# A fifth load buffer for two passes of a Fourier-layer kernel, and a transposed tile that moves into the ring of rectified chunks

## The chip, the cores and the metric

The kernel runs on one core of a Trainium2 chip. The metric is the device time of one execution in microseconds (us); three executions of the kernel before give 11959.6, 11963.65 and 11971.61 us, so the median is 11963.65 us. One more execution was taken with the hardware profiler; the profile and every trace view below come from that one.

## What is computed

The reference takes 64 images of 256 x 256 points. Four Fourier layers turn each into 32 channels and mix them; then one transformer layer runs over the 256 rows of the image and 77 text tokens. Only the Fourier layers matter here:

```
v = [x, gx, gy] @ p_w + p_b                       # 32 channels, per point
for i in range(4):
    x_ft = rfft2(v)                               # only 12 y and 2*12 x frequencies are kept
    out1 = einsum('bixy,ioxy->boxy', x_ft[:, :, :12, :12], W1)
    out2 = einsum('bixy,ioxy->boxy', x_ft[:, :, -12:, :12], W2)
    x1 = irfft2(out_ft, s=(256, 256))
    x2 = einsum('bcxy,cd->bdxy', v, w_w[i]) + w_b[i]
    v = batch_norm(x1 + x2)                       # mean and variance over all 64 images
    if i < 3: v = relu(v)
```

The mean and variance are over the whole batch, so a layer cannot be finished for any image before its statistics are known for all of them. The kernel computes those from the frequencies and from the squares of the channel product, in a stage of its own.

## The kernel before

**Stages.** A first stage computes the frequencies of the input. Then come, three times, a mixing stage (`mix`, lines 392 to 493) and a pass over all images (`layer`, lines 508 to 750); a fourth mixing stage and the transformer end the kernel. A pass computes the layer's output for every image, rectifies it, writes it to DRAM, and transforms it forward for the layer after. Pass i = 0 rebuilds its input from the image itself; the passes i = 1 and i = 2, called the later passes here, read the channels that the pass before wrote, 8 MB an image, and write as much again.

**Chunks.** An image is worked on in eight chunks t = 0..7 of 128 partitions x 8 x 256 floats, 1 MB each. The order of all instructions in a pass is the order in which the code issues them (`tc.manual_schedule()`). Step (b, t) of the loop at lines 721 to 747 does:

- `pre(b, t)`: TensorE sums the inverse transform (line 616) and, in the later passes, the product of the loaded chunk `vin` with the weights (line 627) in PSUM. Half of the result is rectified by ScalarE (line 634) and half by VectorE (line 639; ScalarE at line 637 for t = 6) into a tile `vo`. SyncE issues the store of `vo` (line 640).
- in the later passes, `load_v`: SyncE issues the load of a later chunk into a tile `vin` (line 581). Its queue holds stores and loads in the order of the code.
- `product` of the chunk before (line 659), whose squares ScalarE sums (line 666).
- `turn(b, t)`: VectorE transposes `vo` into a tile `t32` (line 647).

**What lies between the chunks.** At t = 2 the products of chunks 0 and 1 are held back, and the forward transform along y of the image before (`along_y`, line 676) stands in their place: 256 matrix multiplies. Its PSUM result is read by VectorE and, by way of a copy `half` on ScalarE (line 686), by VectorE again (line 688): both transposes go into the tile `zt`. At t = 3 `along_x` (line 701) reads `zt`, and ScalarE and SyncE write the 72 KB of frequencies out (lines 708 and 709). `spread` (lines 598 and 602) runs at t = 3 and t = 5.

**Buffers.** A pool hands out its buffers in turn; a tile may be written when all users of the tile that had the buffer before are done. Pool `li` has two buffers of 16 KB a partition in pass 0, and four of 8 KB in the later passes (`vin`). Pool `lo` has four of 8 KB (`vo`). Pool `lz` holds one `zt` (8 KB) and one `half` (4 KB). Pool `lt` holds six `t32` (16 KB each). With the others they fill the SBUF nearly to its end. PSUM holds four tiles `ring` of two banks; `pre`, `product` and `along_y` take two tiles each, `spread` and `along_x` one.

**Between two passes.** The next mixing stage reuses the addresses. GpSimd issues the loads of the mixing weights into tiles `wn` (line 369), clears and fills part of the weight tile `wm` (lines 374 and 375), and issues the load of the frequencies of 56 images, `xh`, 4 MB (line 769), all on one queue in order. The order on that queue is chosen by the framework's scheduler, not written by hand. TensorE's first product of `mix` (line 419) needs `xh`.

Of the kernel before, what the change touches and what calls it, by code (L numbers as in the profile page):

```python
# [9 lines left out]
F32 = mybir.dt.float32  # L10
# [6 lines left out]
S = 256  # L17
C = 32
# [117 lines left out]
def tile_fno_fusion_transformer(ctx: ExitStack, tc: tile.TileContext, a, cst_d, grid_d, out):  # L136
# [371 lines left out]
    def layer(i, st, src, dst, acc):  # L508
# [7 lines left out]
        with ExitStack() as cx:  # L516
            def pool(name, bufs, **kw):
                return cx.enter_context(tc.tile_pool(name=name, bufs=bufs, **kw))

            ip = pool("li", 2 if i == 0 else 4, reuse_waits="tile")  # L520
            op, yp, cp, xp, zp, tp = (
                pool(n, k, reuse_waits="tile")
                for n, k in (("lo", 4), ("ly", 1), ("lc", 1), ("lx", 2), ("lz", 1), ("lt", 6))
# [39 lines left out]
            y_, t32, vin, vo = {}, {}, {}, {}  # L563

            def load_am(b):
                for n in range(2):
                    nc.sync.dma_start(
                        ams[b % 2][64 * n:64 * n + 2 * KX],
                        mix_d[i][b].rearrange("p k c -> (p k) c")[:, 512 * n:512 * n + 512],
                    )  # L570

            def load_x(b):
                for n in range(4):
                    nc.sync.dma_start(
                        mv[b % 2][32 * n + 24:32 * n + 28],
                        x[b].rearrange("(j n s) y -> n j s y", j=4, n=4)[n],
                    )

            def load_v(b, t):
                vin[b, t] = ip.tile([128, 8, S], F32, name="vin")  # L580
                nc.sync.dma_start(vin[b, t], src[b][:, t])
# [10 lines left out]
            def spread(b, h):  # L592

                y_[b, h] = yp.tile([128, 32, C], F32, name=f"y{h}")
                ps = pp.tile([128, 2, 512], F32, name="ring")
                for n in range(2):
                    hv = slice(64 * n, 64 * n + rows_)
                    nc.tensor.matmul(  # L598
                        ps[:, n, :], lhsT=EX[hv, 128 * h:128 * h + 128], rhs=ams[b % 2][hv],
                        start=True, stop=True, skip_group_check=True,  # L600
                    )
                nc.vector.transpose(  # L602
                    y_[b, h].rearrange("p q c -> p c q"), ps.rearrange("p n (c k) -> p (n c) k", k=32)
                )

            def four():

                t2 = [pp.tile([128, 2, 512], F32, name="ring") for _ in range(2)]
                return t2, [t2[n // 2][:, n % 2] for n in range(4)]

            def pre(b, t):
                t2, ps = four()
                for r in range(2):
                    for n in range(4):
                        q = 8 * (t % 4) + 4 * r
                        nc.tensor.matmul(  # L616
                            ps[n][:, 256 * r:256 * r + 256],
                            lhsT=y_[b, t // 4][32 * n:32 * n + K, q:q + 4, :].rearrange("p q c -> p (q c)"),
                            rhs=mv[b % 2][32 * n:32 * n + K, 2 * t + r, :] if i == 0 else T4[32 * n:32 * n + K, :],
                            start=r == 0, stop=i == 0, skip_group_check=True,  # L620
                        )
                if i:
                    v = vin.pop((b, t))
                    for k in range(4):
                        for n in range(4):
                            j = (n + k) % 4
                            nc.tensor.matmul(  # L627
                                ps[n][32 * j:32 * j + 32], lhsT=ws[32 * n:32 * n + 32],
                                rhs=v[32 * n:32 * n + 32, 2 * j:2 * j + 2, :], start=False, stop=True,
                                skip_group_check=True, tile_position=(32 * n, 32 * j),  # L630
                            )
                o = vo[b, t] = op.tile([128, 8, S], F32, name="vo")
                of = o.rearrange("p (n r) y -> p n (r y)", r=2)
                nc.scalar.activation(of[:, 0:2], t2[0], AF.Relu)  # L634

                if t == 6 or i == 0 and t == 1:
                    nc.scalar.activation(of[:, 2:4], t2[1], AF.Relu)  # L637
                else:
                    nc.vector.tensor_scalar(of[:, 2:4], t2[1], 0.0, None, ALU.max)  # L639
                nc.sync.dma_start(dst[b][:, t], o)  # L640

            def turn(b, t):

                o = vo[b, t]
                if t % 2 == 0:
                    t32[b, t // 2] = tp.tile([128, 8, 16, C], F32, name="t32")
                nc.vector.transpose(  # L647
                    t32[b, t // 2][:, :, 8 * (t % 2):8 * (t % 2) + 8, :].rearrange("p y s c -> p s y c"),
                    o.rearrange("p s (y l) -> p s y l", l=32),
                )  # L650

            def product(b, t):

                o = vo.pop((b, t))
                t2, ps = four()
                for k in range(4):
                    for n in range(4):
                        j = (n + k) % 4
                        nc.tensor.matmul(  # L659
                            ps[n][32 * j:32 * j + 32], lhsT=w4[i + 1][32 * n:32 * n + 32],  # L660
                            rhs=o[32 * n:32 * n + 32, 2 * j:2 * j + 2, :], start=True, stop=True,
                            skip_group_check=True, tile_position=(32 * n, 32 * j),
                        )
                for n in range(2):
                    at = 2 * (8 * b + t) + n
                    nc.scalar.activation(t2[n], t2[n], AF.Square, accum_out=acc[:, at:at + 1])  # L666

            zts = {}

            def along_y(b):  # L670
                t2, ps = four()
                for k in range(8):
                    for m in range(4):
                        for n in range(4):
                            j = (n + m) % 4
                            nc.tensor.matmul(  # L676
                                ps[n][32 * j:32 * j + 32], lhsT=FYT[32 * n:32 * n + 32, k, :],
                                rhs=t32[b, j][32 * n:32 * n + 32, k].rearrange("p s c -> p (s c)"),
                                start=k == 0, stop=k == 7, skip_group_check=True,
                                tile_position=(32 * n, 32 * j),  # L680
                            )
                for j in range(4):
                    t32.pop((b, j))
                zt = zts[b] = zp.tile([128, 2, 32, C], F32, name="zt")
                half = zp.tile([128, 2, 512], F32, name="half")
                nc.scalar.copy(half, t2[1])  # L686
                for h, s2 in enumerate((t2[0], half)):
                    nc.vector.transpose(  # L688
                        zt[:, h].rearrange("p k c -> p c k"),
                        s2.rearrange("p n (s c) -> p c (n s)", c=C),  # L690
                    )
# [21 lines left out]
            if i == 0:  # L713
                load_x(0)
            else:
                for t in range(4):
                    load_v(0, t)
            scale_am(0)
            spread(0, 0)
# [1 line left out]
            for b in range(B):  # L721
                for t in range(8):
                    pre(b, t)
                    nb, nt = (b, t + 4) if t < 4 else (b + 1, t - 4)
                    if i and nb < B:
                        load_v(nb, nt)
                    hold = b > 0 and t in (1, 2)
                    if not hold and (b or t):
                        product(*((b, t - 1) if t else (b - 1, 7)))
                    if t == 3:  # L730
                        spread(b, 1)
                        if b + 2 < B:
                            load_am(b + 2)
                    if t == 5 and b + 1 < B:
                        spread(b + 1, 0)
                    turn(b, t)
                    if hold and t == 2:

                        along_y(b - 1)
                        product(b, 0)  # L740
                        product(b, 1)
                    if b and t == 3:
                        along_x(b - 1)
                    if i == 0 and t == 0 and b + 1 < B:
                        load_x(b + 1)
                    if t == 7 and b + 2 < B:
                        scale_am(b + 2)
# [411 lines left out]
```

## Time and profile before

The profiled execution took 11961.02 us, of which 11959.2 us lie between its first and its last instruction (the span); the other 1.8 us are around it. The median of the three unprofiled executions is 2.6 us longer.

| | us | share of the span |
|---|---|---|
| TensorE, matrix multiplies | 11022.9 | 92% |
| VectorE | 8507.8 | 71% |
| ScalarE | 6492.7 | 54% |
| GpSimd | 1327.1 | 11% |
| stretch 3300:5900 (inside pass 1): TensorE busy | 2426.41 of 2600.00 | granted clock 1.00, DMA 0.92, 358 GB/s |
| stretch 6200:8900 (inside pass 2): TensorE busy | 2519.72 of 2700.00 | granted clock 1.00, DMA 0.92, 358 GB/s |
| stretch 299:2990 (most of pass 0): TensorE busy | 2538.55 of 2691.00 | granted clock 0.98, DMA 0.61, 226 GB/s |

How to read it: busy time is the time in which an engine has an instruction running, and one that it spends waiting is not counted. A row of the table of waits reads "engine and line that waited <- what released it: us in total, times, longest". A wait with the releaser "issue" is time in which the engine waited for nothing that the profile shows. The DMA figure is the mean busy share of the core's 16 DMA engines. Pass 1 begins with its first chunk at 2926.93 us and pass 2 at 6124.66 us.

### The profile page before, as it was taken

The numbers are of one execution on the slowest core, as the hardware profiler recorded it, in microseconds if no ns is written. First come the engines' busy times: TensorE is split into PE (matmuls) and PEld (weight loads), VectorE is DVE, ScalarE is ACT, GpSimd is POOL, SyncE is SP. The second block draws the span as 40 slices with busy tenths as digits, with TensorE's granted clock in tenths as the row PEclk, the third lists the DMA queues.
The fourth block names the chain that finished last, engine by engine and source line by source line (L and its number), as shares of the span: only waits on it lengthen the run. The fifth ranks groups of instructions, "written<-read, shape, count | busy, mean of one in ns | idle before, by whom it ended". The sixth has DMA issues, their size and how long they took to land. (4 is left out here: it accounts for less than half of the span.)

```text
span 11959.2 us, 405306 instructions
## 1 busy us (share of the span) xinstructions
PE 11022.9 (92%) x182038; PEld 5966.9 (50%) x182038; DVE 8507.8 (71%) x10405; ACT 6492.7 (54%) x10697; POOL 1327.1 (11%) x1987
## 2 busy tenths in 40 slices
PE   6999999996999999999969999999997799999998
PEld 3444444443444444444434444444444566666666
DVE  5877878876777777777766777777766666666665
ACT  5666666665555555555545555555555333333333
POOL 0000000001000000000010000000001133333333
PEclk7999999998999999999979999999998899999999
DMA  7555555557999999999988999999998665555553
GB/s 230 224 223 217 223 223 220 223 222 261 354 353 354 360 361 356 362 362 357 356 306 348 360 359 361 357 356 360 359 356 311 255 236 217 233 221 230 224 225 145
DMA packets 589286, 3485.09 MB, mean 291 GB/s; under 512 B 95001, under 2 KB 144537, under 8 KB 188569
## 3 DMA queue, kind: packets, MB, share of 16 engines
q1 hardware_dynamic: 539520, 3392.84, 73.2%
q0 software_dynamic: 40880, 62.59, 2.1%
q8 instruction: 1425, 23.35, 0.8%
q10 hardware_dynamic: 7144, 3.72, 0.1%
q14 instruction: 317, 2.59, 0.1%
HBM read 1761.87 MB, written 1696.92 MB: 289 GB/s over the span
## 5 line engine op out<-in xcount | busy, mean ns | idle before, releaser
L647 DVE STREAM_TRANSPOSE t<-vo 128x2048 f32<-128x2048 f32 x1536 | 3526.4, 2299 | 190.5 <-ACT vo L637 78.9
L666 ACT ACTIVATE ring<-ring 128x1024 f32<-128x1024 f32 x3072 | 3112.7, 1013 | 363.2 <-PE ring L659 300.4
L659 PE MATMUL ring<-vo,w 32*32 32x512 f32 x49152 | 2671.7, 603 | 97.6 <-issue 61.4
L634 ACT ACTIVATE vo<-ring 128x1024 f32<-128x1024 f32 x1536 | 1567.9, 1021 | 1039.1 <-PE ring L627 956.0
L676 PE MATMUL ring<-t,cst 32*32 32x512 f32 x49152 | 1868.1, 599 | 224.6 <-issue 223.9
L639 DVE TENSOR_SCALAR vo<-ring 128x1024 f32<-128x1024 f32 x1280 | 1550.0, 1211 | 611.4 <-PE ring L627 523.2
L676 PEld LDWEIGHTS ring<-t,cst 32*32 32x32 f32 x49152 | 981.9, 103 | 1036.4 <-issue 648.1
L659 PEld LDWEIGHTS ring<-vo,w 32*32 32x32 f32 x49152 | 823.0, 103 | 1348.0 <-issue 612.6
L616 PE MATMUL ring<-cst,y 24*128 24x256 f32 x16384 | 1413.7, 404 | 59.1 <-ACT vo L637 27.9
L616 PEld LDWEIGHTS ring<-cst,y 24*128 24x128 f32 x16384 | 904.7, 185 | 954.2 <-ACT vo L634 458.6
L586 POOL TENSOR_TENSOR ams<-ams,bns 48x512 f32<-48x512 f32 x384 | 400.9, 1044 | 8252.9 <-DMA ams<-mix 7556.5
L627 PE MATMUL ring<-vin,ws 32*32 32x512 f32 x32768 | 1201.4, 603 | 62.3 <-DMA vin<-v 61.2
L686 ACT COPY half<-ring 128x1024 f32<-128x1024 f32 x192 | 194.3, 1012 | 1812.9 <-PE ring L676 1812.9
L688 DVE STREAM_TRANSPOSE zt<-ring 128x1024 f32<-128x1024 f32 x192 | 373.2, 1944 | 1033.8 <-PE ring L676 1033.8
L602 DVE STREAM_TRANSPOSE y<-ring 128x1024 f32<-128x1024 f32 x384 | 755.5, 1967 | 483.2 <-PE ring L598 483.2
L616 PE MATMUL ring<-mv,y 29*128 29x256 f32 x8192 | 746.2, 408 | 44.1 <-ACT ring L666 22.0
L616 PEld LDWEIGHTS ring<-mv,y 29*128 29x128 f32 x8192 | 465.9, 185 | 474.4 <-ACT vo L634 167.2
L701 PEld LDWEIGHTS ring<-cst,zt 128*128 128x128 f32 x4608 | 535.4, 194 | 156.8 <-issue 140.7
L666 ACT ACTIVATION_READ_ACCUMULATOR ring<-ring 128x1 f32 x3072 | 584.9, 190 | 0.0
L1108 POOL DMA_DIRECT2D out_dram<-o x1024 | 504.5, 501 | 658.8 <-DVE o L1103 627.9
L701 PE MATMUL ring<-cst,zt 128*128 128x96 f32 x4608 | 567.6, 280 | 8.2 <-DVE zt L688 8.2
L598 PE MATMUL ring<-ams,cst 49*128 49x512 f32 (+1 forms) x1536 | 452.5, 642 | 38.3 <-POOL ams L586 29.1
(367 smaller groups left out, 9901.3 us busy)
## 6 DMA issues: line engine op xcount, KB each, us to landing
v<-vo SPq DMA_DIRECT2D x1536, 1024.0 KB
vin<-v SPq DMA_DIRECT2D x1024, 1024.0 KB
ch<-v SPq DMA_DIRECT2D x512, 1024.0 KB
mix<-ob SPq DMA_DIRECT2D x96, 512.0 KB
ams<-mix SPq DMA_DIRECT2D x384, 96.0 KB
xin<-in_x_dram SPq DMA_DIRECT2D x16, 1024.0 KB
mv<-in_x_dram SPq DMA_DIRECT2D x256, 64.0 KB
out_dram<-o POOLq DMA_DIRECT2D x1024, 16.0 KB, 3.0
```

Source lines behind the costliest of these rows:

```text
L598: nc.tensor.matmul(ps[:, n, :], lhsT=EX[hv, 128 * h:128 * h + 128], rhs=ams[b % 2][hv], start=True, stop=True, skip_group_check=True,)
L602: nc.vector.transpose(y_[b, h].rearrange("p q c -> p c q"), ps.rearrange("p n (c k) -> p (n c) k", k=32))
L616: nc.tensor.matmul(ps[n][:, 256 * r:256 * r + 256], lhsT=y_[b, t // 4][32 * n:32 * n + K, q:q + 4, :].rearrange("p q c -> p (q c)"), rhs=m ...
L627: nc.tensor.matmul(ps[n][32 * j:32 * j + 32], lhsT=ws[32 * n:32 * n + 32], rhs=v[32 * n:32 * n + 32, 2 * j:2 * j + 2, :], start=False, sto ...
L634: nc.scalar.activation(of[:, 0:2], t2[0], AF.Relu)
L639: nc.vector.tensor_scalar(of[:, 2:4], t2[1], 0.0, None, ALU.max)
L647: nc.vector.transpose(t32[b, t // 2][:, :, 8 * (t % 2):8 * (t % 2) + 8, :].rearrange("p y s c -> p s y c"), o.rearrange("p s (y l) -> p s ...
L659: nc.tensor.matmul(ps[n][32 * j:32 * j + 32], lhsT=w4[i + 1][32 * n:32 * n + 32], rhs=o[32 * n:32 * n + 32, 2 * j:2 * j + 2, :], start=Tru ...
L666: nc.scalar.activation(t2[n], t2[n], AF.Square, accum_out=acc[:, at:at + 1])
L676: nc.tensor.matmul(ps[n][32 * j:32 * j + 32], lhsT=FYT[32 * n:32 * n + 32, k, :], rhs=t32[b, j][32 * n:32 * n + 32, k].rearrange("p s c -> ...
L701: nc.tensor.matmul(ps[:, 0, 96 * g:96 * g + 96], lhsT=zt[:, h, k0:k0 + 4, :].rearrange("p k c -> p (k c)"), rhs=FX[:, h, 48 * r:48 * r + 9 ...
L1108: nc.gpsimd.dma_start(out[b, 64 * n + 16 * g:64 * n + 16 * g + 16].rearrange("(p t) d -> p t d", t=2), o[32 * g + 8 * n:32 * g + 8 * n + 8 ...
```

## The change

Two edits in `layer`:

```diff
-            ip = pool("li", 2 if i == 0 else 4, reuse_waits="tile")
+            ip = pool("li", 2 if i == 0 else 5, reuse_waits="tile")
...
-                zt = zts[b] = zp.tile([128, 2, 32, C], F32, name="zt")
+                zt = zts[b] = op.tile([128, 8, S], F32, name="vo").rearrange(
+                    "p (h k a) (b c) -> p h (k a b) c", h=2, k=4, c=C
+                )
                 half = zp.tile([128, 2, 512], F32, name="half")
...
-                for t in range(4):
+                for t in range(5):
                     load_v(0, t)
...
-                    nb, nt = (b, t + 4) if t < 4 else (b + 1, t - 4)
+                    nb, nt = (b, t + 5) if t < 3 else (b + 1, t - 3)
                     if i and nb < B:
                         load_v(nb, nt)
```

In the later passes the pool of loaded chunks has five buffers, a pass begins with five loads, and step (b, t) issues the load of the chunk five steps on instead of four. In all three passes `zt` no longer has a buffer of its own: it takes the next of the four `vo` buffers, so an image takes nine places in that ring instead of eight. No instruction is added or dropped on any engine; a wait on a store is added to the first transpose into `zt`, and addresses shift by 8 KB: in the later passes those of the tiles between `li` and `half`, in pass 0 those of `half` and `t32`. Line numbers after line 684 grow by two.

## The prediction

> **What bounds the kernel now.** I read the page first (slices and groups), then the table of waits, then TensorE's timeline, the DMA stretches, SyncE's issues, and last the seam between two passes.
>
> ```profile
> PE   6999999996999999999969999999997799999998
> DMA  7555555557999999999988999999998665555553
> q8 instruction: 1425, 23.35, 0.8%
> ```
>
> TensorE is busy nearly everywhere. In the later passes (slices 10 to 30) DMA is nearly full too.
>
> ```profile
> PE ring L676 <- issue: 223.9, 177, 4.4
> PE ring L627 <- DMA vin<-v: 61.2, 78, 2.1
> ```
>
> The second row is what five buffers can remove: 61.2 us, 0.5%. The first is larger: in `along_y` TensorE waits for nothing that the profile shows. Two images in a row:
>
> ```profile
> 4512.34 1.15 PE L627 MATMUL ring<-vin,ws 32*32 32x512 f32 x32 [1.17 <-DMA vin<-v]
> 4513.23 6.69 PE L676 MATMUL ring<-t,cst 32*32 32x512 f32 x184
> 4520.51 2.77 PE L676 MATMUL ring<-t,cst 32*32 32x512 f32 x69 [0.59 <-issue]
> ...
> 4559.73 1.15 PE L627 MATMUL ring<-vin,ws 32*32 32x512 f32 x32 [0.24 <-DMA vin<-v]
> 4567.42 3.84 PE L676 MATMUL ring<-t,cst 32*32 32x512 f32 x102 [1.20 <-issue]
> 4573.64 2.18 PE L659 MATMUL ring<-vo,w 32*32 32x512 f32 x41 [1.76 <-issue]
> ```
>
> The load wait stands always at t = 2, just ahead of `along_y`. Where it was 1.17, the unnamed gaps after it come to 0.59; where it was 0.24, to 1.20 + 1.76.
>
> ```profile
> 4526.00:4528.00 2.00, 1.87 (x32) 0.44 (x15) 1.31 (x1) 0.94 (x3) 0.00 (x0) 1.00 1.01 426
> 4528.00:4530.00 2.00, 2.00 (x50) 1.03 (x48) 0.00 (x0) 2.00 (x4) 0.00 (x0) 1.00 0.51 209
> 4530.00:4532.00 2.00, 2.00 (x36) 0.53 (x32) 1.22 (x1) 1.65 (x3) 0.00 (x0) 1.00 0.08 33
> ```
>
> The last two columns are DMA share and GB/s. Once an image, about 13 us after the last issue (4515.52), DMA runs empty for some 3 of 48 us. So DMA is not the bound over an image; it only lags in the burst t = 0, 1, 2, where a chunk takes 3.7 us (4504.19 to 4507.88 between two stores) and a store and a load, 2.1 MB, take 5 us at 420 GB/s.
>
> **What the Trainium skill says.** "Runtime: NRT & Kernel Launch", Instruction fetch mechanics: instructions come in blocks of 16 KiB, 256 of them, over a DMA queue of the engine's own, the next block while the current one runs. The trace agrees on the size: 23.35 MB in 1425 packets, 16 KB each. Where one gap follows another in `along_y`, 128 products and their 128 weight loads lie between, 4.45 us of work, and the second gap is 1.49 or 1.76 us: a block then takes 5.9 to 6.2 us to come. A plain chunk uses 256 instructions in 3.7 x 256 / 160 = 5.9 us, so it gives the fetch no lead; a load wait does. "DMA: Bandwidth & Descriptors", Queues, rings and completion order: each DMA engine takes queues in turn by packet, so a data queue that is never empty slows the fetch at any depth. In pass 0, with DMA at 0.61, these gaps nearly vanish (2.3 us on L676 from 400 to 2900). "Perfetto Trace Analysis", Optimization Strategy: a bubble that repeats can mean too few buffers. The load wait is one; the fetch gap is not.
>
> **The change part by part.**
>
> *Five loads ahead.* Each step issues the same store and load at the same place; only the loaded chunk is one later. So DMA's timetable stays, and every load lands one store and load, about 5 us, earlier against its need. The longest wait is 2.1 us: all 61.2 us go. What comes next is the fetch. I took 125 images (all but the ends of the passes) from TensorE's timeline. 47 have no load wait; from their line 627 at t = 2 to the next chunk's line 616 they take 16.21 us. The 37 with a wait over 0.8 us waited 1.20 us on average and then take 15.31 us. So 0.90 of 1.20 us comes back as shorter gaps; a straight line through all 125 gives 0.79 of each us, with a standard error of 0.12. I take 0.75 returned: the change keeps 0.25 x 61.2 = 15 us. Bounds: 0 (the fetch takes everything) and 61 us (it takes nothing).
>
> *The first loads of a pass.* One more load at the start, on SyncE's queue behind the `ams` loads. The first image has no load wait in either pass; its chunk 0 waits for line 602. Cost nothing, hidden by the 8 us that TensorE waits for `ams` there; uncovered it is one issue, 0.5 us a pass.
>
> *`zt` in the ring.* The same transposes of 1.94 us, at other addresses. What is new: the first one waits for the store of chunk 7 of the image before.
>
> ```profile
> 4504.19 0.32 SPq L640 DMA_DIRECT2D v<-vo  x1
> ...
> 4523.49 1.94 DVE L688 STREAM_TRANSPOSE zt<-ring 128x1024 f32<-128x1024 f32 x1 [6.03 <-PE ring L676]
> ```
>
> It was issued 19.3 us earlier. Behind it stood its own load and three more pairs, 7.3 MB, done at about 4529; at 0.42 MB/us the store was done near 4511.5. 12 us of cover, less some 2 us for the receipt (an estimate from "DMA: Bandwidth & Descriptors", Anatomy of one DMA; no row shows a store's landing). The ring also turns faster: chunks 3, 4, 5 now wait for the stores of chunks 0, 1, 2, which have `along_y` between (22 us or more from issue to use), and chunk 6 for `along_x`, done 11 us earlier. The other chunks keep a distance of four. But chunk 2 no longer waits for a load that stood behind the store it needs; by the same count that store is done some 4 us before its eviction. Late by 2 us it would still be hidden behind `along_y`, since VectorE idles 6.03 us there. Cost 0; without the cover, each us late at `zt` stops VectorE, then the products behind it: queued are chunk 1's product, for its PSUM, and all of the next chunk.
>
> *The seam between passes.* Addresses moved, so GpSimd's order changes. After pass 0:
>
> ```profile
> 2817.29 1.06 POOL L374 MEMSET wm<- 128x1152 f32 x1 [22.61 <-DVE fr L407]
> 2818.39 1.15 POOL L375 COPY wm<-w 128x1152 f32<-128x1152 f32 x1
> 2819.48 2.41 POOL L369 DMA_DIRECT2D wn<-in_L_tok_fw_dram  x5
> 2821.88 0.55 POOL L769 DMA_DIRECT2D xh<-xh  x1
> ```
>
> `mix` then starts at 2838.49, after 22.39 us of waiting for `xh`. In the built order of the changed program the clear stands ahead of twelve weight loads instead of five, and it waits, as before, for the last `xo`. Seven more issues of 0.48 us make 3.4 us; the last group also waits for the first of the twelve to land, on which I put 3 us more (the weight loads after pass 1 freed their places 4.4 to 7.8 us after issue). `xh` and all behind it: 6 us later, bounds 3 and 11. After passes 1 and 2 three stand there instead of five: 2 x 0.48 = 1 us earlier each. Sum +4 us, bounds +1 and +9.
>
> Sum: -15 + 4 = -11 us. The profiled execution would go from 11961.02 to about 11950; from the median, 2.6 us above it, 11963.65 - 11 = 11952 us.
>
> **The rivals.**
>
> *A, the wait is all gain.* If the fetch lead is not what shortened those gaps, for instance because images with a late load had a lighter DMA afterwards, all 61 us stay: 11963.65 - 61 + 4 = 11906 us. For: 1.20 and 0.90 are an association, not an experiment. Against: the sum of wait and stretch is 16.2 us without a wait and 16.5 with a long one.
>
> *B, the wait moves to another load.* If DMA were the bound, the lag would come back at the next chunk: no gain, +4 us at the seam, 11968 us. Against: the 3 us in which DMA is empty.
>
> *C, slower: the ring holds `zt`.* If the store of chunk 7 lands later than my count, the first transpose into `zt` waits, in all three passes. From 12 us later it bites; a mean lateness of 0.5 us over the 126 images of the later passes costs 63 us: 11952 + 63 = 12015 us. It turns into a loss from 11 / 126 = 0.09 us. For: no row shows when a store lands. Against: the queue empties at about 4529 with three later pairs in it.
>
> **How the numbers follow.** 0.2% is 24 us, about what a measurement of this kernel can tell from no change. My forecast, 11952, has 0.47; A and what lies between (over 28 of the 61 us kept, so that 24 are left after the seam) 0.38; B 0.05; C and an unseen loss over 24 us 0.10. Faster 0.38, same 0.47 + 0.05 = 0.52, slower 0.10. The range reaches down almost to A, 11910, as its cause is unproven, and up to B with the worse seam, 11975; below and above I leave about one in ten each. The forecast's own range is 11940 to 11963.
>
> **What would show it.** Right: the row of line 627 waiting for a load falls from 61.2 to under 5 us, while the "issue" rows of lines 676 and 659 grow by some 45 us together; VectorE's line 690 has no wait for a DMA; `mix` after pass 0 waits for `xh` some 6 us longer. Wrong: the issue rows stay as they are (A); line 627 still waits (B); line 690 waits for `v` (C).

## The result, and the profile after

Twelve executions of each kernel: 11963.52 us before (11939.9 to 11977.47), 11936.06 us after (11914.0 to 11942.8). The ratio is 0.9976, with a 95% interval of 0.9967 to 0.9984: 0.24% faster, some 29 us (19 to 40). The profiled execution after took 11936.87 us, with a span of 11935.1; the span before was 11959.2, so the profiles differ by 24.1 us.

The slices of the page look as before: TensorE busy nearly everywhere, DMA nearly full in the later passes.

```profile
PE   6999999996999999999969999999997799999998
DMA  7555565567999999999889999999998665655553
```

The answer lies in the groups and in the table of waits. In the group of line 627, the columns after the bar are busy time, mean of one in ns, and idle time before it:

```profile
L627 PE MATMUL ring<-vin,ws 32*32 32x512 f32 x32768 | 1202.3, 603 | 2.6 <-issue 2.6
```

It waited 61.2 us for loads before; now it waits for none (the 2.6 us are "issue"). The waits (total, times, longest):

```profile
DVE vo L690 <- PE ring L676: 1003.6, 192, 11.2
...
PE ring L676 <- issue: 249.6, 188, 2.6
...
PE mps L419 <- DMA xh<-xh: 72.3, 3, 32.3
...
PE ring L659 <- issue: 62.0, 56, 2.0
```

The transposes into the moved tile (line 690) wait for TensorE only, never for a store. The unnamed gaps of `along_y` (line 676) were 223.9 us and are 249.6; those of the products (line 659) were 61.4 and are 62.0. So 26.3 of the 61.2 us came back as gaps. The longest wait for `xh` went from 22.9 to 32.3 us.

Here is one image of pass 1 on TensorE's timeline (start, duration, instruction, and in brackets the idle time before it):

```profile
4508.38 1.14 PE L627 MATMUL ring<-vin,ws 32*32 32x512 f32 x32
4509.26 6.78 PE L676 MATMUL ring<-t,cst 32*32 32x512 f32 x184
4517.79 2.78 PE L676 MATMUL ring<-t,cst 32*32 32x512 f32 x69 [1.75 <-issue]
```

Line 627 starts without a wait, `along_y` runs for 184 products, and then stands 1.75 us. Before, an image with a wait of 1.17 us had a gap of 0.59 us at this place.

The table cuts TensorE's timeline where a pass ends (the first line 504 behind it) and where the mixing ends (line 475):

| stretch | before | after | difference |
|---|---|---|---|
| up to the end of pass 0 | 2815.5 | 2816.4 | +0.9 |
| seam and mixing after pass 0 | 95.4 | 105.3 | +9.9 |
| pass 1 | 3085.3 | 3064.1 | -21.2 |
| seam and mixing after pass 1 | 96.4 | 94.1 | -2.3 |
| pass 2 | 3086.5 | 3073.1 | -13.4 |
| seam and mixing after pass 2 | 109.8 | 108.7 | -1.1 |
| what follows | 2638.3 | 2641.4 | +3.1 |

(The short lead-in from a seam's end to a pass's first line 627 is 16 us in both.)

The table compares one execution of each kernel, and the twelve executions of one kernel spread over 29 to 38 us, so a row of a few us proves nothing by itself. The +0.9 us up to the end of pass 0 and the +3.1 us behind the last seam were not followed up. The two passes give 34.6 us and the seams take 6.5.

The first seam, on GpSimd's timeline after the change (the bracket again is the idle time before the row):

```profile
2818.18 1.06 POOL L374 MEMSET wm<- 128x1152 f32 x1 [63.29 <-DVE fr L407]
...
2820.37 3.85 POOL L369 DMA_DIRECT2D wn<-in_L_tok_fw_dram  x8
2824.41 0.49 POOL L369 DMA_DIRECT2D wn<-in_L_tok_fw_dram  x1 [0.19 <-issue]
...
2830.10 0.55 POOL L771 DMA_DIRECT2D xh<-xh  x1 [1.15 <-DMA wn<-in_L_tok_fw_dram]
```

Twelve weight loads now stand between the clear and the issue of `xh`. That issue comes 11.9 us after the clear's start; before it was 4.6 us (2817.29 to 2821.88). TensorE's first product of the mixing stage starts at 2849.27 instead of 2838.49.

The ends of the passes hold a gain that the prediction had not looked for. The last `along_y` of pass 1 on TensorE's timeline, before:

```profile
5987.33 7.98 PE L676 MATMUL ring<-t,cst 32*32 32x512 f32 x191
5999.72 4.47 PE L676 MATMUL ring<-t,cst 32*32 32x512 f32 x65 [4.40 <-issue]
```

and after:

```profile
5981.09 8.09 PE L676 MATMUL ring<-t,cst 32*32 32x512 f32 x190
5991.21 2.73 PE L676 MATMUL ring<-t,cst 32*32 32x512 f32 x66 [2.03 <-issue]
```

The gap of 4.40 us is 2.03 now. GpSimd's weight loads for the next stage run beside it. Before, eight were issued together from 5985.61, less than 2 us ahead of this `along_y`, and three more in it; after, four went out at 5975.02, seven from 5979.36, and two in it. No run changes this alone; it is read from the traces. At the end of pass 2 the gap falls from 3.86 to 1.44 us. From the start of the last `along_y` to the end of the pass it is 4.2 and 4.7 us less, 8.9 together.

### The profile page after: what moved, and what is told of

Its sections match the earlier page's. It is cut to its first block, busy times and chain, and to the rows that moved or that the text cites. A ratio compares the mean times of both kernels' runs of the same rounds, so it can differ in the third digit from the quotient of the medians.

```text
span 11935.1 us, 405502 instructions
## 1 busy us (share of the span) xinstructions
PE 11028.3 (92%) x182038; PEld 5938.1 (50%) x182038; DVE 8507.9 (71%) x10405; ACT 6492.0 (54%) x10697; POOL 1327.3 (11%) x1987
## 3 DMA queue, kind: packets, MB, share of 16 engines
q8 instruction: 1425, 23.35, 0.8%
## 5 line engine op out<-in xcount | busy, mean ns | idle before, releaser
L676 PE MATMUL ring<-t,cst 32*32 32x512 f32 x49152 | 1876.8, 598 | 250.4 <-issue 249.6
L690 DVE STREAM_TRANSPOSE vo<-ring 128x1024 f32<-128x1024 f32 x192 | 373.5, 1945 | 1003.6 <-PE ring L676 1003.6
L703 PEld LDWEIGHTS ring<-cst,vo 128*128 128x128 f32 x4608 | 533.8, 193 | 156.2 <-issue 142.1
L703 PE MATMUL ring<-cst,vo 128*128 128x96 f32 x4608 | 566.0, 280 | 8.6 <-DVE vo L690 8.6
```

The costliest lines, as they stand in the source:

```text
L676: nc.tensor.matmul(ps[n][32 * j:32 * j + 32], lhsT=FYT[32 * n:32 * n + 32, k, :], rhs=t32[b, j][32 * n:32 * n + 32, k].rearrange("p s c -> ...
L703: nc.tensor.matmul(ps[:, 0, 96 * g:96 * g + 96], lhsT=zt[:, h, k0:k0 + 4, :].rearrange("p k c -> p (k c)"), rhs=FX[:, h, 48 * r:48 * r + 9 ...
```

## The experiments

The theory to test, as the prediction has it: `along_y` uses up instructions faster than they are fetched beside a full DMA queue; the time that TensorE waits for a load just ahead of it is a lead for the fetch, so removing the wait lengthens the gaps behind. The rivals: the wait and the gaps have nothing to do with each other (A); the moved `zt` or the new addresses make the difference (C and the seam); and, found on the way, that time ahead of `along_y` helps only because DMA has got further by then. Where a time is compared with the changed kernel's, both were set against the kernel before, run beside them, and the difference is that of the two ratios. With the intervals of both ratios, such a difference from the changed kernel is uncertain by 14 to 19 us.

**Loads only four ahead, all else as changed.**

```diff
-                for t in range(5):
+                for t in range(4):
                     load_v(0, t)
...
-                    nb, nt = (b, t + 5) if t < 3 else (b + 1, t - 3)
+                    nb, nt = (b, t + 4) if t < 4 else (b + 1, t - 4)
```

> The changed kernel, but it loads four chunks ahead as before, with all five buffers, the ring and the addresses of the change kept. Fetch theory (a load wait ahead of the y transform gives TensorE's instruction fetch a lead, so taking the wait away gives part of it back as unnamed gaps): line 627 waits some 60 us again, the unnamed gaps of line 676 fall from 250 back to about 224 us, and the time is 20 to 35 us above the changed kernel's, near 11963. If the waits were a plain gain, it is 60 us above it. If the gain came from the new addresses or the ring, it equals the changed kernel.

Measured: 11959.35 us (11942.55 to 11968.29), 0.9996 of the kernel before (0.9988 to 1.0004). Its waits on TensorE:

```profile
PE ring L676 <- issue: 214.6, 176, 2.6
...
PE ring L627 <- DMA vin<-v: 67.0, 86, 2.7
PE ring L659 <- issue: 64.3, 55, 2.0
```

Against the changed kernel the load wait is 67.0 us longer, the gaps are 32.7 us shorter (278.9 against 311.6), and the time is longer by 0.0020 of 11963.5, 24 us (10 to 38). So the earlier loads account for 24 of the 29 us by the medians, and half of the wait that they remove comes back as gaps. The new addresses alone give nothing that the interval separates from no change, and A, which has all of the wait kept, falls.

**The moved tile only: four buffers and loads four ahead, `zt` in the ring.**

```diff
-            ip = pool("li", 2 if i == 0 else 5, reuse_waits="tile")
+            ip = pool("li", 2 if i == 0 else 4, reuse_waits="tile")
```

with the four-ahead lines of the run above.

> The kernel before with one edit: the turned y result takes a place in the ring of rectified chunks; four buffers, four ahead. GpSimd's built order has the clear of the weight tile ahead of twelve weight loads at all three seams, which the changed kernel has only after pass 0. If the ring is free and that order is what costs: the two later passes keep their length within 10 us, line 690 waits for no store, and each of the three seams grows by about 10 us, less some 4 us at the end of each later pass where fewer weight loads run beside the last y transform: 11963 + 30 - 8 = 11985. If the ring itself costs, the passes grow by more than 20 us and a wait for a store shows at line 690, 634 or 639. If the ring is what gained, the passes get shorter by 20 us or more.

Measured: 11975.96 us (11963.79 to 11996.65), ratio 1.0011 (1.0005 to 1.0018), so slower. Line 690 waited for TensorE only, as in the changed kernel: the ring costs no wait, and C falls. The loss lies between the passes: +10.3, +8.8 and +10.4 us, since here twelve weight loads stand ahead of `xh` at all three seams. The passes are 4.6 and 7.6 us shorter, of which 4.5 and 4.9 us lie between the start of the last `along_y` and the end of the pass (gaps of 1.41 and 0.28 us in it, with four weight loads beside it). As far as these rows show, moving the tile acts through the order of GpSimd's queue: it costs at the seam and gives some of it back at a pass's end.

**Work of few instructions ahead of `along_y`.** The changed kernel, with `spread(b, 1)` at t = 2 instead of t = 3: four products and their four weight loads in 1.13 us, where a plain chunk has 160 instructions in 3.7 us.

```diff
-                    if t == 3:
+                    if t == 2:
                         spread(b, 1)
-                        if b + 2 < B:
-                            load_am(b + 2)
+                    if t == 3 and b + 2 < B:
+                        load_am(b + 2)
```

> The changed kernel with the spread of the second half moved from t = 3 to t = 2, ahead of the y transform: eight TensorE instructions that take about 1.06 us, the same work in another place. Fetch theory: it uses few instructions for its time, so the fetch gains about 0.9 us of lead where it is short of it; two thirds of that come out of the gaps, 0.6 us x 190 images at most, so 60 to 110 us less than the changed kernel, about 11860, and the unnamed gaps of line 676 fall from 250 us to 150 or less. If those gaps have another cause (the chip pausing, or records missing in the trace), the gaps stay at 250 us and the time changes by less than 20 us.

Measured: 11796.05 us (11793.38 to 11807.47), ratio 0.9862 (0.9849 to 0.9876): by the ratios 136 us below the changed kernel, with not one instruction fewer. The gaps:

```profile
PE ring L676 <- issue: 157.6, 138, 4.5
```

They are 92 us shorter (just short of the 150 us expected), those of line 659 stay (61.0). The sign was expected, the gain in time is larger than the 60 to 110 us foreseen: some 44 us more than the gaps. The profiled execution, the slowest of the four, is 129 us shorter than that of the changed kernel: 92 us in these gaps, 28 in TensorE's busy time (11000.6 us instead of 11028.3), and 12 in its waits ahead of line 616. VectorE's transpose behind the spread (line 602) moved too, into the time in which it waits for `along_y`; how much of the 44 us is due to that was not separated.

**The same move in the kernel before.**

> The kernel before (four buffers, its own place for the turned y result) with only the spread of the second half moved to t = 2. Against the changed kernel with the same move (11796) it gives the worth of the fifth buffer where the fetch is short of less lead. If the fetch takes back what the load wait gave, the buffer is worth more here than the 27 us of the change: 35 to 60 us, so 11830 to 11855. If the two are independent, it is worth the same 27 us, so 11823.

Measured: 11847.09 us (11839.42 to 11865.71), ratio 0.9909 (0.9895 to 0.9922). Its waits:

```profile
PE ring L676 <- issue: 149.9, 135, 4.4
...
PE ring L627 <- DMA vin<-v: 40.9, 71, 2.7
```

Here a load wait of 40.9 us stands, and the fifth buffer removes it at the cost of 6.1 us of gaps (149.9 + 62.6 against 157.6 + 61.0): 15% comes back. The fifth buffer and its ring are then worth 0.9909 - 0.9862 = 0.0047, 56 us (33 to 79), about twice the 29 us of this case (19 to 40). The two intervals overlap a little, and the 35 us of wait kept do not make up all of the 56, so this run supports the reading that the same edit pays more where the fetch is less short, and does not prove it alone.

**No stores in pass 2.**

```diff
-                nc.sync.dma_start(dst[b][:, t], o)
+                if i < 2:
+                    nc.sync.dma_start(dst[b][:, t], o)
```

> The changed kernel, but pass 2 stores none of its rectified chunks (what is left out: the whole of the pass's output in DRAM). Halving the stores left the queue full beside the y transform, where the gaps are, so it could not tell; without any store one load of 1 MB comes per chunk and the queue runs empty inside the burst. Fetch theory: the DMA share beside the y transform of pass 2 falls well under 1.0, and the unnamed gaps of line 676 in pass 2 fall from 112 us to under 30 us, while those of pass 1 stay near 100. If the gaps have nothing to do with DMA, they stay in pass 2 as well.

Measured, in one execution: 11716.6 us. Lines move by one: `along_y` is 677 here. Waits in pass 1, from 3300 to 5800 us, which still stores:

```profile
PE ring L677 <- issue: 106.0, 82, 2.0
```

and in pass 2, from 6200 to 8900 us:

```profile
PE ring L677 <- issue: 12.0, 19, 1.8
```

DMA's share is 0.92 in the first stretch and 0.53 in the second, TensorE's program the same. So the gaps of line 676 fall to about a tenth where the DMA queue is no longer full. Pass 2 took 2846.2 us where pass 1 took 3079.6. Of these 233 us the gaps of both lines make some 145: 106.0 + 23.6 us in 2500 against 12.0 in 2700, each taken to the length of its pass. The rest was not placed.

**Half of each store in pass 2.** The store writes only half of every chunk there.

```diff
-                nc.sync.dma_start(dst[b][:, t], o)
+                nc.sync.dma_start(dst[b][:, t], o) if i < 2 else nc.sync.dma_start(dst[b][:, t, 0:4], o[:, 0:4])
```

> The changed kernel, but pass 2 stores only half of each rectified chunk (what is left out: the other half of the pass's output in DRAM). Pass 1 is as before, so it is the control inside the run. Fetch theory: DMA in pass 2 falls from 0.92 to about 0.7 busy, a block of instructions comes sooner, and the unnamed gaps of line 676 in pass 2 fall from about 125 us to under 40 us while those of pass 1 stay; pass 2 gets 100 to 180 us shorter. If the gaps have nothing to do with DMA, pass 2's gaps and length stay as pass 1's.

Measured, in one execution: 11885.01 us; DMA's share in pass 2 falls to 0.75, but line 676's gaps there stay at 111.7 us (113.0 in the changed kernel). A miss, and the windows of one image say why. TensorE's timeline has this gap:

```profile
7656.86 2.22 PE L676 MATMUL ring<-t,cst 32*32 32x512 f32 x40 [2.59 <-issue]
```

and in windows of 2 us around it the last two columns are DMA share and GB/s:

```profile
7652.00:7654.00 2.00, 2.00 (x74) 1.03 (x60) 0.01 (x1) 0.00 (x0) 0.00 (x0) 1.00 0.98 408
7654.00:7656.00 2.00, 0.28 (x12) 0.00 (x0) 0.00 (x0) 0.00 (x0) 0.00 (x0) 1.00 0.97 399
7656.00:7658.00 2.00, 1.14 (x38) 0.61 (x40) 0.00 (x0) 0.00 (x0) 0.00 (x0) 0.97 0.42 178
```

DMA is full until less than 1 us ahead of the gap's end (0.92 from 7655 to 7656 us, 0.52 in the next); what the smaller stores free lies behind it. In keeping with this, the gaps of line 659, which come after `along_y`, did fall in pass 2, from 26.7 to 8.2 us. The mean share of a pass says nothing on the stretch that is short.

**More of the same wait: loads three ahead.** As the first run, with `range(3)` and `(b, t + 3) if t < 5 else (b + 1, t - 5)`.

> The changed kernel, loading only three chunks ahead: a larger dose of the same wait. Each load lands about 5 us later against its need than with four ahead, so the load wait at t = 2 rises from some 0.5 to 4 or 5 us an image (500 to 650 us in all). Fetch theory: such a wait lets the fetch get a full block ahead; the gaps of line 676 fall from 250 to under 110 us, but no further, so that only some 1 to 1.5 us an image comes back and the rest is lost: 11936 + 350 to 500, near 12360. If a wait and the gaps have nothing to do with each other, the gaps stay near 250 us.

Measured: 12518.69 us (12507.78 to 12524.41), ratio 1.046 (1.0442 to 1.0477).

```profile
PE ring L627 <- DMA vin<-v: 571.3, 371, 3.6
PE ring L676 <- issue: 78.2, 95, 2.3
```

The gaps fall by 171 us, and line 659's by 20 to 42.3: with more waiting, fewer gaps, as the lead theory has it. The time is some 160 us above the 12360 that the expectation worked out. What it had not counted came with it: TensorE's clock fell, as the last section shows, and the same products took 210 us longer (11238.4 us busy instead of 11028.3). The wait of 571 us, less 191 us of gaps, plus these 210, makes 590; the profiled executions differ by 587.5.

**Dense work ahead of `along_y`.** All the runs above mix two things: what puts time ahead of `along_y` gives the fetch a lead, and also lets the data queue get further. Here the product of chunk 0 is no longer held back, so it stands ahead of `along_y`: 32 products and 32 weight loads in 1.49 us, as dense as a plain chunk.

```diff
-                    hold = b > 0 and t in (1, 2)
+                    hold = b > 0 and t == 2
...
                         along_y(b - 1)
-                        product(b, 0)
```

> The changed kernel, with one of the two held products no longer held: the product of chunk 0 goes out at t = 1 again, ahead of along_y instead of behind it. So along_y starts about 1.5 us later against the stores and loads of the burst, but the work put ahead of it is as dense in instructions as a plain chunk (32 products and 32 weight loads in 1.49 us), so it gives the instruction fetch no lead. Lead theory (the time ahead of along_y helps because the next block of instructions comes in meanwhile): gaps of line 676 stay near the 250 us of the changed kernel, within 25, and the time within 30 us of it. Drain theory (it helps because the data queue has got further by then): gaps fall as they did where the spread was moved by 1.1 us, by 90 us or more, and the time falls by 60 us or more below the changed kernel's 11936.

Measured: 11918.79 us (11916.97 to 11932.58), ratio 0.9964 (0.9951 to 0.9977), 14 us below the changed kernel by the ratios, which their intervals do not separate from none.

```profile
PE ring L676 <- issue: 264.3, 194, 2.6
```

`along_y` starts later against the burst, by the 1.49 us of the product where the spread takes 1.13, and its gaps do not shrink: 264.3 against 249.6. In the profile pass 0, which has next to no gaps, is 18.6 us shorter, and the later passes together 15 us longer. So what helps is not that `along_y` comes later, but that few instructions are used just ahead of it. And on top of the moved spread:

> The same in the kernel that has the spread ahead of along_y (11796 us, gaps of line 676 157.6 us). Lead theory: gaps stay at 135 to 180 us and the time within 30 us of 11796. Drain theory: along_y then starts 2.6 us later against the burst than in the changed kernel, gaps fall below 90 us and the time to about 11730.

Measured: 11782.75 us (11777.09 to 11790.52), ratio 0.9851 (0.9835 to 0.9867), with gaps of 150.0 us on line 676 against 157.6: again as the lead theory has it. It is the fastest of the kernels run, though its interval overlaps with that of the moved spread alone.

**Both spreads ahead of `along_y`,** with two buffers for `y0`, and `xh` loaded on SyncE's queue. This and the next run looked for a faster kernel.

```diff
-                y_[b, h] = yp.tile([128, 32, C], F32, name=f"y{h}")
+                y_[b, h] = yp.tile([128, 32, C], F32, name=f"y{h}", bufs=2 - h)
...
-                    if t == 3:
+                    if t == 2:
                         spread(b, 1)
-                        if b + 2 < B:
-                            load_am(b + 2)
-                    if t == 5 and b + 1 < B:
-                        spread(b + 1, 0)
+                        if b + 1 < B:
+                            spread(b + 1, 0)
+                    if t == 3 and b + 2 < B:
+                        load_am(b + 2)
...
-                    nc.gpsimd.dma_start(
+                    nc.sync.dma_start(
```

> As the run before, and the spread of the next image's first half moves from t = 5 to t = 2 as well (one more buffer of 4 KB a partition for its result). Fetch theory: another 0.9 us of lead ahead of each y transform; the gaps of line 676 fall from 158 us to under 90, and the time by 30 to 90 us more, to about 11710. If the lead cannot grow further because the fetch is only one block ahead, it changes by less than 20 us.

Measured: 11958.97 us (11954.37 to 11975.87), ratio 1.0 (0.9992 to 1.0008), a miss by 250 us. The gaps fell to 98.7 us, but a new wait is there:

```profile
PE ring L676 <- DVE vo L639: 74.9, 63, 1.2
```

`along_y` now waits for the PSUM tile that VectorE has still to evict. Almost all of this wait, 72.4 us, is in pass 0, where there were no gaps to save, and that pass ends at 2934.8 us instead of 2816.4. The later passes are 10 and 18 us longer than with one spread moved (the next run), although their gaps are shorter; why was not followed up.

**The moved spread with `xh` on SyncE's queue** (the last two lines of that diff, in the kernel with one spread moved).

> The changed kernel with the spread moved to t = 2 and the early load of xh issued by SyncE instead of GpSimd, so that it no longer stands behind weight loads at the seams. The first product of the mixing stage then waits for the weight tile instead: 72 us of waiting for xh become about 45 us over the three seams, seam 1 falls from 105 to about 90 us, seams 2 and 3 by some 6 us each: 11796 - 27 = 11769. If the weights, not xh, set the start of the products, the seams stay and so does the time.

Measured: 11804.77 us (11797.03 to 11811.51), ratio 0.9873 (0.9858 to 0.9888): no gain over the 0.9862 without it, where the expectation had 27 us.

```profile
PE mps L419 <- DVE wm L388: 81.4, 4, 32.5
```

The wait for `xh` is gone, and a wait for the weight tile took its place, with the same longest one (32.5 us, at the first seam): there the weights are as late as `xh`.

## Why the prediction was right, and which terms were off

The forecast was 11952 us and the measurement is 11936.06, 4 us below the forecast's own range, in the stretch that the prediction left between its forecast and rival A. The sign and the mechanism held, but the sum had 11 us of the 29: some three fifths of the gain were missing from it.

- *All 61.2 us of the load wait go.* They do; line 627 waits for no load.
- *0.75 of it is returned as gaps, 15 us stay.* The mechanism is shown from four sides: with four loads ahead the gaps are shorter, with three ahead shorter still, without stores they all but vanish, and dense work ahead of `along_y` doesn't shorten them while sparse work does. The records of the packets, below, show it directly. The size: over the 125 images counted in the prediction the wait falls from 0.456 us an image to none, and the stretch from line 627 at t = 2 to the next line 616 grows from 15.90 to 16.20 us: 67% returned. That is within the error of 0.12 on which I took 0.75, and leaves about 19 us of the 57 in these images.
- *Missing from the sum: the rest of the pass.* The same images save another 0.05 us each outside that stretch, some 7 us in all, for which I have no cause. The pass ends save 8.9 us, by the weight loads that GpSimd issues earlier. The prediction asked what the new order on GpSimd does behind the pass, and never what it does to the last `along_y` beside it. The term "keeps 15 us" was thus 34.6 us in the passes. In the rows of the waits the return is 26.3 us and not the 45 foreseen. The shorter gaps at the two ends, 4.8 us, stand in the same rows; without them the rows give about one half returned where the stretch gives 67%, and this difference was not placed.
- *The seams: +6, -1, -1.* They came to +9.9, -2.3 and -1.1. At the first, the seven more issues and their waits for landings made 7.3 us, where I put 3.4 + 3. The other 2.6 us are the transfer itself: from issue to first product 19.2 us instead of 16.6. A later issue was counted as a mere shift; it also took longer.
- *`zt` in the ring costs nothing.* Right: line 690 waits for no DMA in any run with it, and the run of that part alone shows no store wait either. One thing is added all the same, against what the description of the change says: a semaphore instruction of 21 ns on VectorE ahead of each of the 192 first transposes, in time in which it waits for TensorE. The estimate of 12 us of cover was not tested further; the 2 us that it takes off for the receipt are given, where the prediction cites them, for transfers that GpSimd issues, and these stores are issued by SyncE.
- *The rivals.* A needed 57 us of gain and got half. B needed a wait on another load, and there is none. C needed a store wait, and there is none.

"Runtime: NRT & Kernel Launch", Instruction fetch mechanics, says in the Trainium skill that crossing into the next block is mostly hidden. In pass 0 the trace agrees, with 2.3 us of gaps. In the later passes it doesn't: the run without stores in pass 2 has 106.0 us in 2500 in pass 1, with DMA at 0.92, and 12.0 us in 2700 in pass 2, with DMA at 0.53.

That the gaps are instruction fetch can be read from the trace itself. No row of the views names them, but the trace holds the start and the end of each of the 1425 packets of queue q8, and TensorE's instructions can be counted in order of time. In the kernel before, TensorE stands idle over 0.4 us ahead of a product of lines 676 and 659 in 213 places. In 210 of them the instruction behind the gap is number 256 i + 449 of TensorE's order, where i is the number of a packet (both counted from 0), with the same 449 from the first gap to the last; and the product that ends the gap starts 1.2 to 1.8 us (median 1.40) after packet i has ended. A gap without a link to the packets would stand at such a place in one case of 256. After the change this holds for 218 of 221. So these gaps stand exactly where one block of 256 instructions ends and the next begins, and they end when that next block has come.

The packets also show what a busy DMA does to the fetch. The third column is the median time from the start of the block before on TensorE to the start of the packet, the last the median time that the packet took:

| kernel and stretch (us) | DMA share | until the packet starts | the packet |
|---|---|---|---|
| before, pass 0 (400 to 2800) | 0.59 | 0.96 | 0.97 |
| before, pass 1 (3300 to 5800) | 0.92 | 3.46 | 0.95 |
| before, pass 2 (6200 to 8900) | 0.92 | 3.57 | 0.96 |
| without stores in pass 2, pass 2 | 0.53 | 1.01 | 0.96 |
| half of each store in pass 2, pass 2 | 0.75 | 2.14 | 0.96 |

The packet itself takes the same time everywhere; what grows is the wait until it starts. Where one gap of `along_y` follows another, 3.8 us of this wait, 0.94 of the packet and 1.4 behind it make the 5.9 to 6.2 us of the prediction. The gaps at the pass ends fit as well: before, the packet started 6.4 us after the block before it at both ends; after, 3.7 and 3.6 us.

What stays open: why moving the spread gave 44 us more than its gaps, and what the 0.05 us an image are. That the packet waits because the data queue's packets go ahead of it fits the table; the trace does not show the order in which a DMA engine chose.

## What to carry to other kernels

Before you remove a wait, look at what the stretch behind it is short of: idle time ahead of it may be feeding that. Here a fifth buffer lost about half of the wait that it removed, while eight sparse instructions moved ahead of the dense stretch, with nothing removed, gave nearly five times as much as this change. And when a tile moves, compare the order of the loads in the stages on both sides, and look at the work beside them as well as behind them.

## What the runs showed of the hardware that I had not expected

- *Short waits can cost the clock.* With loads three ahead, TensorE's clock was 0.94 over 3300 to 5900 us, where the changed kernel had 1.00. On the timeline one image waits 2.65 us for a load at 4550.40; in windows of 2 us (the third column from the right is the granted clock):

```profile
4551.00:4553.00 2.00, 0.00 (x0) 0.00 (x0) 2.00 (x1) 0.00 (x0) 0.00 (x0) 1.00 1.06 446
4553.00:4555.00 2.00, 1.95 (x34) 0.65 (x35) 0.16 (x1) 0.00 (x0) 0.00 (x0) 0.51 0.96 406
4555.00:4557.00 2.00, 2.00 (x58) 1.05 (x61) 1.62 (x2) 1.02 (x1) 0.00 (x0) 0.64 1.07 446
```

  The clock is halved for 3.4 us after the wait is over. The Trainium skill, "TensorE: Matmul & The Clock Gate", What's actually happening, describes a clock of one half after an idle window of about 3.4 us. Here an idle time of 2.65 us, after a wait of 1.33 us that had ended 2.2 us before it, was enough. So in that run a wait costs more than its own length.
- *DMA can be full and slow.* Beside the weight loads at the end of pass 1, DMA's share was 0.98 at 213 GB/s (5995 to 6000 us, before), where the prediction's window from 4526 to 4528 us has 426 GB/s at a share of 1.01. That is where the gap of 4.40 us stood, the longest of line 676.
- *TensorE's instructions come one block ahead at most.* In the kernel before, no packet of q8 started while more than 301 instructions were still to run ahead of the first that it holds. By this count, time gained more than a block ahead of a dense stretch cannot be stored up; what helped here stood just ahead of it.
